# The last expert's weighting, sum and output of the last chunk in two halves, on a kernel whose order is planned

## The chip, the cores and the metric

One core of a Trainium2 chip runs the whole kernel. The time is the device time of one execution in microseconds (us). It is given as the median of several runs. A trace is one profiled execution, whose span goes from the first to the last recorded instruction.

The engines are named as the profile names them: PE is TensorE (matrix multiplies and transposes; PEld is its weight load), DVE is VectorE, ACT is ScalarE, POOL is GpSimd, and SP is SyncE, which here only issues DMAs. Each engine runs its own queue of instructions in order and waits on semaphores for the others. A "q" behind a name (SPq, ACTq) means the engine's sequencer, for instance while it issues a DMA.

## What is computed

The input is x with two batches, 1024 steps and 128 channels. Four layers follow, each behind a layer normalization and added to x:

```python
x = x + attn_a(layernorm(x))   # a linear recurrence with a decay per channel
x = x + ffn(layernorm(x))
x = x + attn_b(layernorm(x))   # 16 heads with an 8x8 state, MLPs in front and behind
x = x + ffn(layernorm(x))      # the same weights again
```

The part that the change touches is the second ffn, a dense mixture of 8 experts with 512 inner features. Every token runs through every expert:

```python
router_probs = softmax(x @ w_router)
gate_weights = softmax(x @ w_gating / 0.1)
h = silu(einsum('bsh,ehf->ebsf', x, w_gate)) * einsum('bsh,ehf->ebsf', x, w_up)
expert_out = einsum('ebsf,efh->ebsh', h, w_down)
cw = router_probs * gate_weights
cw = cw / (cw.sum(-1) + 1e-9)
out = einsum('ebsh,bse->bsh', expert_out, cw)
```

## The kernel before, in words

**Chunks and layers.** Time is cut into five chunks: four of 192 steps and a last one of 256. Both batches lie side by side, so a chunk is 384 columns wide, the last one 512. The residual x of a chunk stays in SBUF as `k.x`, with 128 tokens on the partitions and one slot of 128 channels for each block of tokens: three slots in the first four chunks, four in the last. In the last chunk two slots belong to each batch. Each chunk passes attn A, the first ffn (f), attn B and the second ffn (g). Attn B's recurrence runs step by step through its chunks on DVE, POOL and ACT, beside the experts, which keep PE busy. `ORDER` (line 84) names the sequence of experts: F0 to F4, then G0 to G4, so g4 is the last work of the kernel.

**One ffn.** `gating` (line 1096) normalizes and transposes x to channels on partitions, makes the experts' weights cw and writes them to DRAM. `experts` (line 1152) takes each expert in four slices of 128 inner features. For one slice PE makes gate and up, each with three matmuls in split precision (`mm3`, line 807), in two PSUM tiles; ACT applies Silu to the gate; DVE (for some slices POOL) multiplies it with up; and PE multiplies the result by the down weights (`down`, line 1159), three slices behind. Gate, up and the down sum share four PSUM tiles ("g", `PSG`). After an expert's fourth slice, `add(e)` (line 1170) reads the broadcast weight `cb` by DMA and multiplies the expert's result with it into a tile `de` (`ds` for expert 0). For most experts that is a copy on ACT and a product on POOL; for the last expert it is one DVE product from PSUM. The products are summed in `ds`.

**The end of g4.** `APART` (line 117) holds "g4". There the sum of experts 0 to 6 is transposed back to tokens on partitions and added to `k.x` by itself (lines 1185 to 1187), beside the last expert's matmuls. The last expert's product is then transposed in four blocks (`transposed`, line 992, line 1192) and added (line 1193). `store` (line 1593) issues one output DMA for each batch of the chunk, as `blocks` (line 765) yields them, both on SP's queue.

**Who sets the order.** No engine call in the kernel's body emits an instruction at once. `Program` (lines 369 to 677) records each call as a step with its engine, its tiles and the steps it depends on, and a list scheduler (`order`, line 486) then simulates the engines with a price list of its own (`_cost`, lines 425 to 484) and picks, for each engine, the ready step of lowest rank. All instructions are emitted from line 677, so every row of the profile carries L677, and rows are told apart by their tiles. The rank is:

```python
far[s.index] = tail(s) + max([far[o.index] for o in s.after], default=0.0)
s.rank = -far[s.index] - s.lead + spread * s.index
```

`far` is the step's longest path to the end of the program at the planner's prices. The lead is a table by part and chunk (`LEAD`, line 71), the spread 427.5 ns for each place in the recorded order. The price of a DVE product or sum of n columns is n / 0.96 + 145 ns (line 452), so 678 for 512 columns and 412 for 256; a transpose of 128 columns is 112 + 195 = 307.

**Which steps depend on which.** Two steps depend on each other where one writes what the other touches. In SBUF the planner compares the ranges within a tile. For a PSUM tile that TensorE and another engine use it takes the whole tile (lines 413 to 417):

```python
for o, ow, olo, ohi, om in tile.steps:
    if (w or ow) and o is not s:
        if psum and "T" in (o.engine, s.engine):
            s.deps.add(o)
        elif lo < ohi and olo < hi and om & m:
            s.deps.add(o)
```

The names in the profile: `g_at` is one of the four PSUM tiles of gate, up and down; `m_at` one of the two other PSUM tiles; `h_at` the Silu and the product; `de_at`, `ds_at`, `cb_at` as above; `x_at` the residual; `wgu_at`, `wd_at` experts' weights; `Zt_at`, `y_at`, `ox_at`, `ot_at`, `pm_at`, `q_at`, `bu_at`, `pz_at`, `xne_at`, `s_de_at`, `s_kr_at` belong to attn B.

Of the kernel before, what the change touches and what calls it, by code (L numbers as in the profile page):

```python
# [35 lines left out]
ALU = mybir.AluOpType  # L36
# [4 lines left out]
E, FF = 8, 512  # L41
EH = 153
ET = EH - 128
P = 128
# [72 lines left out]
APART = "g4".split()  # L117
# [563 lines left out]
def hybrid_kernel(  # L681
# [21 lines left out]
    nc = Program(tc.nc)  # L703
# [21 lines left out]
    def psum(name, w=W, ring=None):  # L725
        pool, tag = ring or ((ps_e, "e" if PSE else "m") if late[0] else (ps_m, "m"))
        return pool.tile([P, W], F32, tag=tag, name=name)[:, 0:w]
# [9 lines left out]
    def chunk(c, t0, tc):  # L737
        k = SimpleNamespace(c=c, t0=t0, tc=tc, w=B * tc, nt=B * tc // P)
        k.qt = tc // 4
        k.ns = k.qt // L  # L740
        k.nseg = 4 * k.ns
        return k

    chunks = [chunk(c, sum(CHUNKS[:c]), tc) for c, tc in enumerate(CHUNKS)]
# [11 lines left out]
    ident = cst[:, 0:P]  # L756
# [8 lines left out]
    def blocks(k, far):  # L765

        for b in range(B):
            q, end = b * k.tc, (b + 1) * k.tc
            while q < end:
                p, n = q % P, q // P  # L770
                t = k.t0 + q - b * k.tc
                m = (end - q) // P
                if p == 0 and m:
                    yield k.x[:, n : n + m, :], far[b, t : t + m * P, :].rearrange("(n p) d -> p n d", p=P)
                    q += m * P
                else:
                    r = min(P - p, end - q)
                    yield k.x[p : p + r, n, :], far[b, t : t + r, :]
                    q += r
# [27 lines left out]
    def mm3(to, w, v, start=True, stop=True):  # L807
        (wh, wl), (vh, vl) = w, v
        nc.tensor.matmul(to, wl, vh, start=start, stop=False)
        nc.tensor.matmul(to, wh, vl, start=False, stop=False)  # L810
        nc.tensor.matmul(to, wh, vh, start=False, stop=stop)
# [23 lines left out]
    def expert_stage(e):  # L835
        st = early(f"wst_{e}", [P, 2, FF])
        nc.sync.dma_start(st[:, 0], w_gate[e])
        nc.sync.dma_start(st[:, 1], w_up[e])
        return st

    def expert_weights(e, f, name, stage):

        t = w2p.tile([P, 2, 2, P], F32R, tag="wgu", name=f"wgu_{name}_{e}_{f}", bufs=NWGU)
        if (e, f) in wcut:
            nc.sync.dma_start(t.bitcast(F32), wcut[e, f])
            return t
        src = stage[:, :, f * P : (f + 1) * P]
        nc.scalar.copy(t[:, 0], src)
        nc.vector.tensor_tensor(t[:, 1], src, t[:, 0].bitcast(F32), ALU.subtract)
        wcut[e, f] = dram.tile([P, 2, 2, P], F32, name=f"wcut_{e}_{f}", bufs=1)  # L850
        nc.sync.dma_start(wcut[e, f], t.bitcast(F32))
        return t

    def down_weights(e, name):

        src = w_down[e].rearrange("p (k h) -> p k h", k=4)
        t = w2p.tile([P, 4, C], F32, tag="wd", name=f"wd_{name}_{e}")
        nc.sync.dma_start(t, src)
        return t
# [76 lines left out]
    def either(site, usual):  # L936

        return nc.vector if vector(site, usual) else nc.gpsimd

    def vector(site, usual):  # L940
        SITES[site] = usual
        return (usual == "V") != (site in ENG)
# [49 lines left out]
    def transposed(k, src, name):  # L992

        pt = psum(f"pt_{name}", k.w)
        for n in range(k.nt):
            nc.tensor.transpose(pt[:, n * P : (n + 1) * P], src[:, n, :], ident)
        return pt

    def tiles(k, ap):
        return ap.rearrange("p (n d) -> p n d", n=k.nt)  # L1000
# [151 lines left out]
    def experts(k, name, gated):  # L1152

        w = k.w
        xc, weight = gated
        queue = []
        s = SimpleNamespace(done=0, pd=None, sum=None)

        def down():
            wt, h = queue.pop(0)  # L1160
            f = s.done % 4
            if f == 0:
                s.pd = ps_d.tile([P, W], F32, tag=DT, name=f"pd_{name}_{s.done // 4}")[:, 0:w]
            nc.tensor.matmul(s.pd, wt, h, start=f == 0, stop=f == 3)
            s.done += 1
            if f == 3:
                with nc.ahead(AHEAD):
                    add(s.done // 4 - 1)

        def add(e):  # L1170

            cb = weight(e)
            d = w2p.tile(
                [P, W], F32, tag="de" if e else "ds", name=f"de_{name}_{e}", bufs=NDE if e else 1
            )[:, 0:w]
            if vector(f"dm_{name}{e}", "V" if e == E - 1 else "P"):
                nc.vector.tensor_tensor(d, s.pd, cb, ALU.mult)
            else:
                nc.scalar.copy(d, s.pd)
                nc.gpsimd.tensor_tensor(d, d, cb, ALU.mult)  # L1180
            if e == 0:
                s.sum = d
            elif e < E - 1:
                either(f"ds_{name}{e}", "P").tensor_tensor(s.sum, s.sum, d, ALU.add)
                if e == E - 2 and name in APART:
                    po = transposed(k, tiles(k, s.sum), f"d{name}s")
                    nc.vector.tensor_tensor(k.x, k.x, tiles(k, po), ALU.add)
            else:
                if name not in APART:
                    nc.vector.tensor_tensor(s.sum, s.sum, d, ALU.add)  # L1190
                    d = s.sum
                po = transposed(k, tiles(k, d), f"d{name}")
                nc.vector.tensor_tensor(k.x, k.x, tiles(k, po), ALU.add)

        for e in range(E):
            nc.part = name.upper()
            stage = None if (e, 0) in wcut else expert_stage(e)
            wd = down_weights(e, name)
            for f in range(4):
                wt = expert_weights(e, f, name, stage)  # L1200
                pg = psum(f"pg_{name}_{e}_{f}", w, (ps_g, GT))
                mm3(pg, (wt[:, 0, 0], wt[:, 1, 0]), xc)
                pu = psum(f"pu_{name}_{e}_{f}", w, (ps_g, GT))
                mm3(pu, (wt[:, 0, 1], wt[:, 1, 1]), xc)
                h = w2p.tile([P, W], F32, tag="h", name=f"h_{name}_{e}_{f}", bufs=NH)[:, 0:w]
                with nc.ahead(AHEAD):
                    nc.scalar.activation(h, pg, AF.Silu)
                    if 4 * e + f in HPOOL.get(name, ()):
                        u = w2p.tile([P, W], F32, tag="h", name=f"u_{name}_{e}_{f}", bufs=NH)[:, 0:w]
                        nc.scalar.copy(u, pu)  # L1210
                        nc.gpsimd.tensor_tensor(h, h, u, ALU.mult)
                    else:
                        nc.vector.tensor_tensor(h, h, pu, ALU.mult)
                    queue.append((wd[:, f, :], h))
                if len(queue) > BEHIND:
                    down()
            if e == E - 1:
                while queue:
                    down()
            nc.part = ""  # L1220
            yield
# [369 lines left out]


    def store(k):
        for tiled, steps in blocks(k, out):
            nc.sync.dma_start(steps, tiled)

    gated, rec, res = {}, {}, {}
    made = {("X", 0): 1}
# [93 lines left out]
    for name in ORDER:  # L1692
        layer, k = name[0].lower(), chunks[int(name[1])]
        ensure(layer, k.c)
        for _ in experts(k, f"{layer}{k.c}", gated[layer, k.c]):
            now += 1
            give()
        made[layer.upper(), k.c] = 1
        give()
        if layer == "g":  # L1700
            store(k)
# [68 lines left out]
```

## Time and profile before

| what | value |
|---|---|
| median of 3 runs | 769.29 us (767.77 to 771.74) |
| the profiled execution's own time | 767.02 us |
| its span, first to last instruction | 765.2 us |
| mean granted TensorE clock | 0.984 |
| PE busy | 718.2 us, 94% of the span |
| DVE busy | 605.8 us, 79% |
| ACT busy | 457.8 us, 60% |
| POOL busy | 430.7 us, 56% |
| DMA | 152.11 MB, mean 199 GB/s |
| activation table loads on ACT | 64, 1283 ns each |

How to read it. A busy share is a mean over stages with different limits, so the page also cuts the span into 40 equal slices and gives each engine's share of a slice in tenths. The chain that ended last is followed back from the last instruction; its shares say which engine's work, not which engine's waiting, leads to the end. In rows of the timeline an idle time ahead of an instruction stands in brackets, with what ended it. Two short views complete the table. The largest waits of PE (what was waited for, us in total, times, longest):

```profile
engine line waited for: us in total, times, longest us
PE g_at L677 <- ACT h_at L677: 9.5, 9, 5.4
PE m_at L677 <- DVE xn_at L677: 8.9, 2, 8.0
PE g_at L677 <- DVE h_at L677: 8.2, 11, 2.3
PE m_at L677 <- DVE bias_at L677: 3.0, 1, 3.0
PE g_at L677 <- POOL h_at L677: 2.3, 1, 2.3
```

And the two stretches in which the granted clock fell in the middle of the kernel (window, length, busy us and count of PE, PEld, DVE, ACT, POOL, granted clock, DMA share, GB/s):

```profile
405.60:409.00 3.40, 0.73 (x6) 0.41 (x4) 3.40 (x4) 3.00 (x8) 2.00 (x2) 1.00 0.71 196
409.00:412.40 3.40, 0.62 (x2) 0.62 (x3) 3.37 (x9) 3.08 (x10) 3.32 (x6) 0.50 0.44 108
412.40:415.80 3.40, 3.40 (x13) 2.68 (x12) 3.40 (x9) 0.98 (x2) 0.23 (x1) 0.50 0.16 34
467.00:470.40 3.40, 1.58 (x6) 0.94 (x6) 3.37 (x13) 3.37 (x6) 3.24 (x7) 1.00 0.41 103
470.40:473.90 3.50, 2.48 (x4) 1.40 (x5) 3.50 (x8) 3.48 (x6) 3.50 (x5) 0.51 0.31 109
473.90:477.30 3.40, 3.39 (x9) 1.90 (x7) 3.04 (x7) 3.13 (x6) 3.40 (x4) 0.50 0.00 0
477.30:480.70 3.40, 3.35 (x22) 3.23 (x23) 3.35 (x9) 2.19 (x4) 3.09 (x5) 1.00 0.38 83
```

### The profile page before, as it was taken

What the parts mean: (1) busy time and instruction counts of PE and PEld (TensorE: products, weight loads), DVE (VectorE), ACT (ScalarE), POOL (GpSimd) and SP (SyncE); (2) the same over time, 40 slices, a digit from 0 to 9 for tenths busy, and PEclk for the clock granted to TensorE, in tenths of its full rate; (3) what the DMA queues carried; (4) which work ended last, traced back from release to release, by engine and by line L of the source; (5) the groups of instructions that cost most, each with busy time, mean ns of one, the idle gap of its engine ahead of it and who ended that gap; (6) DMA issues with size and microseconds to landing.
All of it is one profiled execution on the core that took longest, in us unless ns stands there. A gap on an engine that the chain in (4) does not pass through costs nothing.

```text
span 765.2 us, 11738 instructions
## 1 busy us (share of the span) xinstructions
PE 718.2 (94%) x3231; PEld 553.7 (72%) x3231; DVE 605.8 (79%) x1387; ACT 457.8 (60%) x913; POOL 430.7 (56%) x490
## 2 busy tenths in 40 slices
PE   4799999899999999999997988999999999999997
PEld 3788887778777878656655755778777777776664
DVE  6675744699999999899999999999999778344332
ACT  3665577648774775643877969655654553554332
POOL 2232332886545497655975589975976247520222
PEclk9799999999999999999998998999999999999999
DMA  7487568676976589855395693686658857746551
GB/s 230 154 286 257 160 182 213 211 207 192 221 216 198 175 218 284 225 169 172 120 235 154 180 311 108 189 257 211 199 179 249 258 163 221 238 134 192 177 166 42
DMA packets 131559, 152.11 MB, mean 199 GB/s; under 512 B 52950, under 2 KB 74518, under 8 KB 131494
## 3 DMA queue, kind: packets, MB, share of 16 engines
q1 hardware_dynamic: 130918, 150.98, 66.8%
q8 instruction: 26, 0.43, 0.2%
q10 hardware_dynamic: 576, 0.38, 0.2%
q14 instruction: 39, 0.32, 0.1%
HBM read 131.79 MB, written 19.53 MB: 198 GB/s over the span
## 4 chain that ended last, share of the span: by engine, by line
PE 46%; DVE 24%; DMA 7%; POOL 7%; issue 6%; ACT 6%; SPq 2%; DVEq 0%; ACTq 0%; POOLq 0%
PE g_at L677 40%; PE m_at L677 7%; DVE h_at L677 5%; DVE bu_at L677 2%; POOL ox_at L677 2%; ACT L677 2%; DVE Z_at L677 2%; DVE pz_at L677 2%; DVE q_at L677 2%; SPq L677 2%; DMA wgu_at<-wcut 2%; ACT h_at L677 1%; DMA d_v<-b_at 1%; DVE ot_at L677 1%; POOL pm_at L677 1%
## 5 line engine op out<-in xcount | busy, mean ns | idle before, releaser
L677 PE MATMUL g_at<-xT_hi_at,wgu_at 128*128 128x384 f32 (+1 forms) x1280 | 483.9, 417 | 16.4 <-ACT h_at L677 9.0
L677 PEld LDWEIGHTS g_at<-xT_hi_at,wgu_at 128*128 128x128 f32 x1280 | 240.1, 190 | 84.1 <-ACT h_at L677 17.5
L677 PE MATMUL g_at<-h_at,wd_at 128*128 128x384 f32 (+1 forms) x640 | 269.1, 512 | 5.5 <-DVE h_at L677 2.7
L677 ACT ACTIVATE h_at<-g_at 128x384 f32<-128x384 f32 (+1 forms) x320 | 162.7, 512 | 185.5 <-PE g_at L677 171.4
L677 DVE TENSOR_TENSOR h_at<-h_at,g_at 128x384 f32<-128x384 f32 (+1 forms) x302 | 172.4, 574 | 98.9 <-PE g_at L677 55.3
L677 PE MATMUL g_at<-xT_lo_at,wgu_at 128*128 128x384 f32 (+1 forms) x640 | 226.6, 354 | 0.0
L677 PEld LDWEIGHTS g_at<-xT_lo_at,wgu_at 128*128 128x128 f32 x640 | 122.3, 191 | 38.9 <-issue 12.5
L677 PEld LDWEIGHTS g_at<-h_at,wd_at 128*128 128x128 f32 x640 | 116.6, 190 | 27.2 <-DVE h_at L677 5.0
L677 POOL TENSOR_TENSOR de_at<-de_at,cb_at 128x384 f32<-128x384 f32 (+1 forms) x50 | 54.8, 1096 | 90.3 <-ACT de_at L677 90.3
L677 ACT ACT_TABLE_LOAD x64 | 82.1, 1283 | 3.7 <-issue 2.6
L677 POOL TENSOR_TENSOR ds_at<-ds_at,de_at 128x384 f32<-128x384 f32 (+1 forms) x58 | 66.3, 1143 | 24.6 <-DVE de_at L677 22.7
L677 POOL TENSOR_TENSOR Z_at<-Z_at,vr_at 128x192 f32<-128x192 f32 (+1 forms) x75 | 49.5, 660 | 34.8 <-DVE Z_at L677 31.7
L677 ACT COPY Zt_at<-Z_at 128x384 f32<-128x384 f32 (+1 forms) x40 | 39.1, 981 | 9.7 <-DVE Z_at L677 7.7
L677 DVE TENSOR_TENSOR q_at<-bu_at,kt_at 128x384 f32<-128x384 f32 (+1 forms) x75 | 43.7, 583 | 0.7
L677 DVE TENSOR_REDUCE bu_at<-pz_at 128x48 f32<-128x384 f32 (+1 forms) x75 | 43.3, 577 | 0.6
L677 POOL TENSOR_TENSOR ox_at<-Zt_at,y_at 128x384 f32<-128x384 f32 (+1 forms) x36 | 40.9, 1152 | 4.8 <-DVE y_at L677 4.6
L677 DVE TENSOR_TENSOR Z_at<-Z_at,q_at 128x384 f32<-128x384 f32 (+1 forms) x75 | 42.8, 571 | 0.8
L677 DVE TENSOR_TENSOR pz_at<-Z_at,bu_at 128x384 f32<-128x384 f32 (+1 forms) x75 | 42.8, 570 | 0.4
L677 ACT COPY de_at<-g_at 128x384 f32<-128x384 f32 (+1 forms) x50 | 24.9, 499 | 27.7 <-PE g_at L677 26.1
L677 POOL TENSOR_TENSOR vr_at<-vt_at,rks_at 128x384 f32<-128x384 f32 (+3 forms) x40 | 35.3, 886 | 1.1
L677 POOL TENSOR_TENSOR om_at<-Z_at,rst_at 128x384 f32<-128x384 f32 (+1 forms) x25 | 32.2, 1286 | 3.6 <-DVE Z_at L677 3.6
L677 POOL TENSOR_TENSOR h_at<-h_at,h_at 128x384 f32<-128x384 f32 x18 | 18.3, 1016 | 17.2 <-ACT h_at L677 17.2
(223 smaller groups left out, 973.0 us busy)
## 6 DMA issues: line engine op xcount, KB each, us to landing
wgu_at<-wcut SPq DMA_DIRECT2D x288, 256.0 KB, 3.1
wd_at<-in_w_down SPq DMA_DIRECT2D x80, 256.0 KB, 2.9
wcut<-wgu_at SPq DMA_DIRECT2D x32, 256.0 KB, 3.8
cb_at<-cd_f SPq DMA_DIRECT2D x32, 192.0 KB, 4.2
cb_at<-cd_g SPq DMA_DIRECT2D x32, 192.0 KB, 3.4
Z_at<-in_w_gate SPq DMA_DIRECT2D x8, 256.0 KB, 2.8
Z_at<-in_w_up SPq DMA_DIRECT2D x8, 256.0 KB
cb_at<-cd_f SPq DMA_DIRECT2D x8, 256.0 KB
```

Source lines behind the costliest of these rows:

```text
L677: getattr(engine, s.call)(*[placed(v) for v in s.args], **{n: placed(v) for n, v in s.kw.items()})
```

## The change

For the last expert of the last chunk of g, `add` no longer multiplies the whole 128x512 result, transposes its four blocks and adds them. It takes one PSUM tile for the transposes and goes through the two batches: for each it multiplies a half (128x256) on DVE, transposes its two blocks and adds the half to `k.x`. `store` sends the second output DMA of the last chunk from ACT's queue instead of SP's. Nothing else in the text of the kernel changes; the order of all steps is planned anew from the recorded ones.

```diff
@@ -1173,6 +1173,16 @@
             d = w2p.tile(
                 [P, W], F32, tag="de" if e else "ds", name=f"de_{name}_{e}", bufs=NDE if e else 1
             )[:, 0:w]
+            if e == E - 1 and k is chunks[-1] and name in APART:
+
+                po = psum(f"pt_d{name}", w)
+                for i in range(2):
+                    ts = slice(i * k.nt // 2, (i + 1) * k.nt // 2)
+                    nc.vector.tensor_tensor(tiles(k, d)[:, ts], tiles(k, s.pd)[:, ts], tiles(k, cb)[:, ts], ALU.mult)
+                    for n in range(ts.start, ts.stop):
+                        nc.tensor.transpose(po[:, n * P : (n + 1) * P], d[:, n * P : (n + 1) * P], ident)
+                    nc.vector.tensor_tensor(k.x[:, ts], k.x[:, ts], tiles(k, po)[:, ts], ALU.add)
+                return
             if vector(f"dm_{name}{e}", "V" if e == E - 1 else "P"):
                 nc.vector.tensor_tensor(d, s.pd, cb, ALU.mult)
             else:
@@ -1591,8 +1601,8 @@
 
 
     def store(k):
-        for tiled, steps in blocks(k, out):
-            nc.sync.dma_start(steps, tiled)
+        for i, (tiled, steps) in enumerate(blocks(k, out)):
+            (nc.scalar if k is chunks[-1] and i % 2 else nc.sync).dma_start(steps, tiled)
```

## The prediction

> **What bounds the kernel now.** I read the page's slices first, to see which engine fills which stage, then the chain that ended last, then windows of 40 us. The slices (each digit tenths of 19.1 us):
>
> ```profile
> PE   4799999899999999999997988999999999999997
> ...
> DVE  6675744699999999899999999999999778344332
> ...
> PEclk9799999999999999999998998999999999999999
> ...
> PE 46%; DVE 24%; DMA 7%; POOL 7%; issue 6%; ACT 6%; SPq 2%; DVEq 0%; ACTq 0%; POOLq 0%
> ```
>
> PE is full nearly throughout; DVE is full from 160 to 560 us; only two dips of PE and of its clock stand in the middle. The windows that decide below (columns: window, its length, busy us and count of PE, PEld, DVE, ACT, POOL, granted clock, DMA share, GB/s):
>
> ```profile
> 400.00:440.00 40.00, 34.32 (x152) 26.36 (x151) 39.28 (x93) 33.60 (x66) 21.22 (x28) 0.91 0.60 175
> 440.00:480.00 40.00, 34.42 (x144) 24.33 (x142) 39.14 (x82) 32.77 (x54) 37.56 (x42) 0.91 0.69 205
> 480.00:520.00 40.00, 38.80 (x181) 30.38 (x182) 39.29 (x87) 23.42 (x52) 33.79 (x33) 1.00 0.78 229
> 520.00:560.00 40.00, 39.10 (x189) 30.81 (x187) 39.70 (x80) 24.77 (x46) 30.85 (x30) 1.00 0.62 193
> 640.00:680.00 40.00, 37.95 (x186) 30.86 (x185) 19.76 (x42) 19.58 (x38) 24.28 (x28) 1.00 0.70 211
> ```
>
> From 440 to 560 us DVE idles 0.86 + 0.71 + 0.30 = 1.87 us in all, so a DVE delay there is not won back. After 640 DVE has 20 of 40 us free, PE 2.05. What the diff names is the end alone (start, us, engine, tile, count, idle before and its releaser):
>
> ```profile
> 759.70 0.69 DVE L677 TENSOR_TENSOR de_at<-g_at,cb_at 128x512 f32<-128x512 f32 x1 [2.73 <-PE g_at L677]
> 760.31 0.68 DVE L677 TENSOR_TENSOR x_at<-x_at,m_at 128x512 f32<-128x512 f32 x1
> ...
> 760.45 0.66 PE L677 MATMUL m_at<-cst_at,de_at 128*128 128x128 f32 x4 [0.40 <-DVE de_at L677]
> 761.14 0.69 DVE L677 TENSOR_TENSOR x_at<-x_at,m_at 128x512 f32<-128x512 f32 x1 [0.15 <-PE m_at L677]
> 761.86 0.90 SPq L677 DMA_DIRECT2D out_x<-x_at  x2
> ```
>
> Weighting, four transposes, sum, two stores in single file; the second store starts 0.44 us after the first (762.30), and the span ends at 765.2, 2.9 us after that. The whole tail the diff can shorten is 765.2 - 759.7 = 5.5 us, 0.7% of the span.
>
> **Part 1: the tail itself.** A DVE row of 128x384 takes 0.55 us and of 128x512 0.69, a slope of 0.14 for 128 elements, so 128x256 is about 0.41. Independent rows overlap by 0.08 (759.70 + 0.69 against 760.31), so two halves start 0.33 apart. The chain after: first mult 759.70 to 760.11, second 760.03 to 760.44; the other experts' sum into x stands behind both on DVE, 760.36 to 761.04; two transposes (0.4 of the 0.66) 760.17 to 760.57; the first half's sum 761.05 to 761.46; its store on SP at 761.49, 0.37 earlier than now. The second half's transposes: the planner counts a PSUM tile as one whole when TensorE and another engine use it (lines 413 to 417), so they wait not only for the second mult but for DVE's first sum; in the built program their wait is on that sum. They run 761.52 to 761.92, the second sum 761.95 to 762.36, the second store on ScalarE's queue at 762.39, where ScalarE has nothing left (its issues at the kernel's start took 0.41 to 0.45, SP's two here 0.39 and 0.46). That is 762.39 against 762.30: **+0.1 us**. Without that wait the two sums would follow each other and the second store go at about 761.85: **-0.45**. With an ACT issue and a wait hop each 0.25 longer: +0.6. I take +0.1: the halves run one after the other, and what the parallel issue saves (0.44) the serial second half gives back. Nothing is queued behind the waiting transposes or the second store.
>
> In the row at 760.31 DVE reads one PSUM tile while PE writes another. No row shows both at once in one tile. The Trainium skill ("PSUM — Partial Sum Buffer", section "PSUM bank collisions raise a hardware error") says that two engines in one bank at once fail rather than queue, which speaks for the wait and against halves in one tile; by it the -0.45 is not to be had without a second tile.
>
> **Part 2: what the tail does to the rest.** The order of all instructions is planned by the kernel: a step's rank (line 503) is minus its longest path to the end, by its own price list (lines 425 to 484). By that list the path from the sum of the other experts to the end was 678 + 678 ns and is now 678 + 412 + 307 + 412, so 453 ns longer. Everything whose longest path runs into the last chunk (its attention, hence all chunks' recurrences) gains 453 ns of urgency against the experts of g0 to g3. In the two built programs PE, DVE, ACT, POOL and SP are identical up to about 414 us of the trace; from there hundreds of places differ on each; they meet again from 561 to 600, and from 692 to the tail. The work is the same but for two DVE halves (+0.3 us in all) and one activation table load (x64 at 1283 ns becomes x65).
>
> To price the new order I gave each instruction the mean duration of its kind in the trace and compared how much work stands ahead of the same instruction in both. That leaves out waits, so it bounds a delay rather than giving it. Two stretches stand out.
>
> *450 to 485 us.* ACT now:
>
> ```profile
> 449.69 0.48 ACT L677 ACTIVATE h_at<-g_at 128x384 f32<-128x384 f32 x1
> 450.37 0.48 ACT L677 COPY h_at<-g_at 128x384 f32<-128x384 f32 x1 [0.19 <-PE g_at L677]
> 451.48 0.49 ACT L677 ACTIVATE h_at<-g_at 128x384 f32<-128x384 f32 x1 [0.63 <-PE g_at L677]
> ```
>
> After the Silu of 449.69 the new order puts a table load (1.28), an Exp of the decay (0.5), two Zt copies (1.87), two PSUM copies (0.96), a third Zt copy (0.92), three xne (1.15), a Square (0.5) and the table load back (1.28): 8.5 us, so the Silu of 451.48 cannot start before 458.6. PE covers some of it with attention matmuls and the four PSUM tiles that gates and ups share, then stands. It stands already now, with waits of
>
> ```profile
> 457.93 0.91 PE L677 MATMUL g_at<-h_at,wd_at 128*128 128x384 f32 x2 [2.28 <-POOL h_at L677]
> 467.43 0.44 PE L677 MATMUL g_at<-xT_hi_at,wgu_at 128*128 128x384 f32 x1 [0.52 <-ACT h_at L677]
> 471.42 2.29 PE L677 MATMUL g_at<-h_at,wd_at 128*128 128x384 f32 x3 [2.29 <-DVE h_at L677]
> ```
>
> so the question is the net. On PE both orders meet at the matmul of 471.42: the same work ahead of it. Its delay is the stretch's delay. Its product, at 463.4 on DVE now, has 8.6 us more DVE work ahead (472.0 + 0.57 = 472.6), its Silu, at 460.60 on ACT, 9.2 us more: at 469.8 if ACT never waits. ACT idles 7.2 and DVE 0.9 of these 40 us, and if ACT waits 2 us in that stretch the matmul starts at 474.6. So +1.2 to +3.2; after it DVE, full until 560, keeps the loss. I take **+2.5**, above the middle because the sum of works leaves waits out; for the range 0 (the Silus after it catch up) to +5 (the decay's data, whose load is issued at 442.20, lands late and holds DVE too).
>
> In the rows PE fell to clock 0.50 from 409.0 to 415.8 and from 470.4 to 477.3, after windows with PE busy 0.73 and 1.58 of 3.4 us, and not after 648.0 to 651.4 with 1.71. Half clock for 6.9 us costs about 3.4. The Trainium skill ("TensorE: Matmul & The Clock Gate", section "Part 1: The HAM clock gate") puts the gate on a free-running window of about 3.4 us, idle or busy; by it the stall that moves here can meet one window more or fewer, 3.4 us either way. My sum keeps one such stretch, as now.
>
> *620 to 652 us.* DVE now runs two products at 624.1 and 624.7; the new order puts 3.5 to 4.9 us of attention work (two 1.2 us rows and the router's small ones) ahead of each, 1.1 by 633.4. PE's cover is what the four shared tiles let it run ahead, one to two slices of an expert; a slice takes 1.74 us (23 records of the down matmul from 500 to 520 us, two to a matmul, as 640 records for 320 slices show). The middle, 4.2 - 2.6, leaves 1.6. At 647.57 a DVE row of 3.67 and one of 0.68 now stand before a product that they followed, so PE's 2.05 wait ending at 651.76 grows by about a slice, 1.7. The two are not added: that row hangs on POOL and DVE, not on the experts, so a PE that is 1.6 late waits 1.6 less for it. **+1.6**; bounds 0 (all covered) and +4 (added, and 0.7 for waits).
>
> *The rest.* 500 to 556 us: products have up to 2.0 us less ahead, but DVE is full and its total is the same: 0. 414 to 450: up to 4.4 more ahead, 0 again by 481: within the first stretch's bounds. The added table load is among the 8.5. SP's issues move with the rest (0.3 to 0.6 each); I price that at 0, since no wait of PE over 0.2 us in the list of waits names a DMA, and DMA is busy 0.69 there; if a load came late it would be in the +5.
>
> **Sum.** +2.5 +1.6 +0.1 = +4.2 us. On the profiled execution's 767.02 that is 771.2; that execution is 2.27 below the median of the runs, 769.29, and on the median it is **773.5 us**, +0.55%.
>
> **Rivals.**
> - *The tail works and the rest is hidden.* Both stretches at 0, the tail between -0.45 and +0.6: 768.8 to 769.9. For it: PE's count of work is the same and both orders meet twice. Against: 8 us on ACT where PE already waits.
> - *The new order takes the stall away* (the other side: faster). If the attention work done early on ACT and DVE at 450 to 461 lets PE pass 467 to 471 without the waits of 0.52 and 2.29, no window falls idle and the half clock of 470.4 to 477.3 goes: -2.8 - 3.4 + 0.1 = -6.1, 763.2. It decides as soon as that product is ready by 469.1, 2.3 us before it is needed now. Against: it has 8.6 us more DVE work ahead, not less.
> - *One half-clock stretch more* on top of my sum: +3.4, 776.9; with all upper bounds (+5, +4, +0.6) 778.9.
> - *The change doesn't do what it says*: the halves do not overlap and the second queue saves nothing. That is already my tail.
>
> **How the numbers follow.** Forecast (delays stand, +0.6 to +7) 0.55; hidden 0.22; stall gone 0.13; more half clock 0.10. A measurement of this kernel tells about 0.5%, 3.85 us. Of the forecast's 0.55 I put 0.40 above that bound. Slower 0.40 + 0.10 = 0.50; same 0.15 + 0.22 = 0.37; faster 0.13. The range goes from 765.0 (both stretches at 0, one half-clock stretch lost, the tail at -0.45: 765.4, rounded down) to 780.0 (the upper bounds and 1 us of the runs' own spread); it leaves out the stall-gone case and half of the last, 0.18.
>
> **What would show it.** Tail: the second half's transposes wait on DVE's x, the second store starts on ACT 2.7 us after the first mult starts (2.6 now). Stretch 1: no Silu between 450.2 and 458.6, a PE wait on ACT of over 2 us there, the 471.42 matmul at 472.6 to 474.6. Stretch 2: a new PE wait on DVE's products near 626 of 1 to 2 us. I am wrong if the 561 us rows come at their old times, or if PE's clock stays 1.00 through 470 to 478.

## The result and the profile after

The changed kernel took 772.92 us (median of 12 runs, 768.68 to 775.17) against 769.89 for the kernel before in the same comparison (12 runs, 766.03 to 772.43): ratio 1.004, 95% interval 1.0021 to 1.0059. It is about 3 us slower. Its profiled execution is its fastest run (768.68, span 766.9), so that page shows less of a loss than the median.

The windows of 40 us that answer to those of before (window, length, busy us and count of PE, PEld, DVE, ACT, POOL, granted clock, DMA share, GB/s); the last line is the kernel before in the window that matters most:

```profile
440.00:480.00 40.00, 34.97 (x152) 25.67 (x151) 39.42 (x87) 33.21 (x53) 37.00 (x42) 0.91 0.68 206
...
600.00:640.00 40.00, 35.02 (x161) 26.34 (x160) 33.72 (x80) 20.35 (x39) 12.13 (x14) 0.96 0.59 178
640.00:680.00 40.00, 39.95 (x196) 32.52 (x195) 20.79 (x45) 20.05 (x39) 27.52 (x28) 1.00 0.70 223
...
600.00:640.00 40.00, 38.52 (x190) 30.59 (x189) 33.50 (x84) 22.47 (x43) 15.15 (x16) 1.00 0.69 209
```

From 440 to 480 us PE's busy time shows no loss: it is even 0.55 us higher. The hole is at 600 to 640 us, where PE falls from 38.52 busy us to 35.02 and its clock to 0.96. Part of it comes back at once: PE is full from 640 to 680, where before it waited 2.05 us.

The clock of 0.96 is one stretch at half clock that before has not. It follows a window in which PE was busy 1.59 of 3.4 us:

```profile
623.70:627.10 3.40, 1.59 (x6) 0.95 (x6) 3.40 (x6) 3.34 (x6) 0.64 (x1) 1.00 0.61 182
627.10:630.50 3.40, 3.20 (x9) 2.62 (x9) 3.40 (x5) 1.02 (x3) 1.72 (x1) 0.50 0.24 74
```

Half clock for 3.4 us is, as an estimate, 1.7 us of PE's work.

To follow the delay along the kernel I took the start of each down matmul in both traces and subtracted; the difference is called the lag below. At 385 us of before, ahead of the first difference, the changed kernel stands at -0.96 us: the two executions differ by chance by that much over identical orders. From there it goes to +8.14 at 461, back to -0.91 at 591, up to +7.01 at 628, and to +1.46 from 694 on. So the first stretch leaves 0.05 us behind, the second 2.37.

The tail, changed kernel (start us, us, engine, tiles, count, idle before and its releaser):

```profile
761.16 0.76 DVE L677 TENSOR_TENSOR de_at<-g_at,cb_at 128x256 f32<-128x256 f32 x2 [2.74 <-PE g_at L677]
...
761.84 1.20 DVE L677 TENSOR_TENSOR x_at<-x_at,m_at 128x512 f32<-128x512 f32 x2
...
763.09 0.44 PE L677 MATMUL m_at<-cst_at,de_at 128*128 128x128 f32 x2 [1.01 <-DVE x_at L677]
763.57 0.42 DVE L677 TENSOR_TENSOR x_at<-x_at,m_at 128x256 f32<-128x256 f32 x1 [0.53 <-PE m_at L677]
764.02 0.41 ACTq L677 DMA_DIRECT2D out_x<-x_at  x1
```

The second half's transposes wait 1.01 us on DVE's sum into x: the halves run one after the other. From the first weighting to the issue of the second output it takes 764.02 - 761.16 = 2.86 us, against 2.60 before: +0.26. From the first weighting to the end of the span it is 5.7 us (766.9 - 761.16) against 5.5 (765.2 - 759.70): +0.2.

### The profile page after: what moved, and what is told of

The parts are those of the page before. It is cut to its first block, busy times and chain, and to the rows that moved or that the text cites. A ratio compares the mean times of both kernels' runs of the same rounds, so it can differ in the third digit from the quotient of the medians.

```text
span 766.9 us, 11750 instructions
## 1 busy us (share of the span) xinstructions
PE 719.5 (94%) x3231; PEld 555.8 (72%) x3231; DVE 606.1 (79%) x1389; ACT 457.9 (60%) x914; POOL 433.8 (57%) x490
## 4 chain that ended last, share of the span: by engine, by line
PE 52%; DVE 25%; ACT 8%; DMA 7%; issue 5%; SPq 1%; POOL 1%; DVEq 0%; ACTq 0%
PE g_at L677 44%; PE m_at L677 7%; DVE h_at L677 5%; DVE bu_at L677 3%; ACT L677 3%; DVE q_at L677 2%; DVE Z_at L677 2%; DVE pz_at L677 2%; DMA wgu_at<-wcut 1%; ACT h_at L677 1%; DMA d_v<-b_at 1%; SPq L677 1%; DMA pm_at<-zd 1%; DVE ot_at L677 1%; DVE cm_at L677 1%
## 5 line engine op out<-in xcount | busy, mean ns | idle before, releaser
L677 POOL TENSOR_TENSOR Z_at<-Z_at,vr_at 128x192 f32<-128x192 f32 (+1 forms) x75 | 51.5, 687 | 32.8 <-DVE Z_at L677 32.4
L677 POOL TENSOR_TENSOR ox_at<-Zt_at,y_at 128x384 f32<-128x384 f32 (+1 forms) x36 | 39.2, 1102 | 4.2 <-DVE y_at L677 3.1
L677 POOL TENSOR_TENSOR h_at<-h_at,h_at 128x384 f32<-128x384 f32 x18 | 19.9, 1103 | 17.9 <-ACT h_at L677 17.8
```

The source lines that it names most:

```text
L677: getattr(engine, s.call)(*[placed(v) for v in s.args], **{n: placed(v) for n, v in s.kw.items()})
```

## The experiments

All ratios are to the kernel before, measured beside it; brackets hold 95% intervals. A ratio is taken over all runs of both kernels and is not the quotient of the two medians. To separate the tail from the order, three lines let a step's share of the planner's longest path be set by hand:

```diff
+        s.path = None
-            far[s.index] = tail(s) + max(...)
+            far[s.index] = (tail(s) if s.path is None else s.path) + max(...)
```

**The tail alone.** The changed text, with the paths of its steps set so that they add up to the old ones. The order is then that of before on PE and POOL throughout, and on the other engines up to the tail.

> The changed tail with the order of before everywhere else (the planner is given the old path lengths for the tail's steps). Theory R, the new order makes the time: ratio 1.000 (within 0.15%), and in the trace only the tail is longer, first weighting to second output 2.8 to 2.9 us against 2.60. Rival T, the halves and the second queue make it: ratio 1.004, the 3 us stand in the tail. Rival N, clock and chance: anything between, with nothing in the tail.

Measured: 0.9999 (0.9976 to 1.0022), and the tail is 2.86 us here too (761.81 to 764.67). The halves and the second queue cost 0.26 us up to the second output and nothing that a ratio can show. Rival T falls.

**The order alone.** The old text, with the last sum's path set to 1438 ns and the last weighting's to -202.

> The old tail with the order of the changed kernel up to it (only the urgency is changed: 760 ns added to the last sum's path, the last weighting's path corrected). Theory R: 1.003 to 1.004 (2.5 to 3 us), and the stretch 620 to 652 us shows the same new waits as in the changed kernel. Rival T: 1.000. Rival N: interval takes in both.

Measured: 1.0059 (1.0038 to 1.0079), medians 773.55 (six runs) against 768.22, and PE waits 0.62, 1.26 and 0.58 us from 628 to 634, as in the changed kernel. The new order alone makes a loss as large as the whole change's, as far as the intervals tell. Rival N falls too: the interval keeps clear of 1. Setting the paths also showed an error of mine. With the 453 ns of my prediction the planner gives another order; with +760 for the last sum and -120 for the last weighting it gives the changed kernel's on every engine up to the tail. All transposes into one PSUM tile depend on each other, so each of them is in the longest path: 678 + 678 became 678 + 412 + 2 x 307 + 412.

**One stretch at a time.** Two kernels are joined from both plans near 585 us, where each engine has emitted the same instructions in both.

```diff
+        a, b = self.planned(True), self.planned(False)
+        done = {s for s in b[0] if b[1][s] < cut}
+        one, two = (a, b) if early else (b, a)
+        out = [s for s in one[0] if s in done] + [s for s in two[0] if s not in done]
```

> Old tail; the changed kernel's order up to the place near 585 us where both orders meet, the order of before behind it. My prediction's first term: +2.5 us, ratio 1.003. What the trace of the changed kernel shows instead (6 us late at 458 to 470, made up by 485, level at 585): 1.000, within 0.8 us.

> Old tail; the order of before up to the place near 585 us, the changed kernel's order behind it. My prediction's second term: +1.6 us, ratio 1.002. What the trace of the changed kernel shows: 6.3 us late at 642, 4 of them made up by 692, +2.4 us left: 1.003. If the two stretches only cost together, both this and the first one are at 1.000 to 1.001.

Measured: the first stretch 1.0016 (0.9992 to 1.0040), 1.2 us, which doesn't exclude 0 nor +2.5; the second 1.0039 (1.0011 to 1.0066), 3.0 us. Over all traces the first stretch (lag at 591 minus lag at 385) leaves 0.05, 1.37, -0.05, 1.75, 0.16, 1.51, 2.24 and 0.68 us in eight kernels that have the new order there, mean 1.0; and 1.49, 0.13, 1.19, -0.41 and -1.55 in five that have the old one, mean 0.2. The second costs, and PE's busy time from 600 to 640 us shows it: 38.5, 37.2, 38.5, 38.3 and 37.6 us in the five traces with the old order there, 35.0, 34.7 and 34.1 in the three with the new one and nothing else moved. The lag alone would not show it in one pair of traces: from 591 to 694 us it grows by 1.87, 1.85, 0.30 and 2.93 us even in the four other traces with the old order there, by 2.37 to 6.73 in the five with the new one and the loads (below) not put back.

The half clock is part of this cost. From 600 to 640 us the mean clock is 1.00 in four of the five traces with the old order and 0.96 in the fifth. It is 0.96 or 0.91 in all eight with the new one, also in those whose loads or Silus are put back below. Over 40 us that is 1.6 or 3.6 us of PE's work (an estimate from the clock alone). No run parts it from the waits that stand ahead of it.

**Two Silus ahead.** In the changed kernel ACT reads so at the start of g3:

```profile
622.79 0.69 ACT L677 COPY si_at<-lm_at 128x128 f32<-128x128 f32 x2 [2.95 <-DMA lm_at<-sd]
623.26 0.54 ACT L677 ACTIVATE h_at<-g_at 128x384 f32<-128x384 f32 x1
623.82 1.28 ACT L677 ACT_TABLE_LOAD   x1
...
626.76 0.87 ACT L677 ACTIVATE h_at<-g_at 128x384 f32<-128x384 f32 x2
```

One Silu goes ahead of the router's table loads, where before three did. I took that order for the cause first.

```diff
+        for n in ("h_g3_0_1", "h_g3_0_2"):
+            move("S", find("S", "activation", n), seq["S"].index(find("S", "activation", "ex_g3")))
+        for n, o in (("h_g3_0_1", "h_g3_0_0"), ("h_g3_0_2", "h_g3_0_1")):
+            move("V", find("V", "tensor_tensor", n), seq["V"].index(find("V", "tensor_tensor", o)) + 1)
```

> The order-only kernel with one edit near 624 us: two Silus of g3's first expert go ahead of the router's Exps and their table load on ACT, and their two products follow the first one on DVE, as in the order of before; nothing else moves. If the second stretch's loss comes from these Silus behind the table loads (theory R in its narrow form): 1.0059 falls to about 1.003, and PE's waits of 0.6, 1.26 and 0.58 us near 628 to 634 shrink to under 1 us in all. Rival, the attention's late data hold ACT and DVE there whatever stands behind: 1.005 to 1.006, and PE waits as long at another row.

Measured: 1.0049 (1.0024 to 1.0073), and PE's waits there are 2.06, 0.58 and 1.63 us: not shorter, only at other rows. The narrow form falls by the waits; the ratio cannot tell it from 1.003. What stands first is the 2.95 us for which ACT waits on a DMA (3.67 in this kernel, 0.69 before), with the Silus behind it.

**A product of the attention on DVE.** In the changed kernel a router row of 3 columns takes as long as a POOL product beside it:

```profile
626.48 2.36 DVE L677 TENSOR_TENSOR dn_at<-su_at 128x3 f32<-128x3 f32 x1
```

```diff
+        s = find("P", "tensor_tensor", "ym_4_1")
+        seq["P"].remove(s)
+        s.engine = "V"
+        seq["V"].insert(seq["V"].index(next(o for o in seq["V"] if o.call == "tensor_reduce" and s in o.deps)), s)
```

> The order-only kernel with one product of the attention (128x1024, 2.4 us on POOL) done on DVE instead, at its place ahead of its reduction. If the router's 3-column row took 2.36 us on DVE because POOL ran that product beside it: the row takes under 0.3 us, the stretch gets 1 us shorter (2.36 - 0.17 - 1.2), ratio 1.004 to 1.005. Rival, the row waits for something else: it stays at 2.4 and the time is 1.007.

Measured: the row takes 0.16 us instead of 2.36, so the cause of its length is shown. The ratio, 1.0035 (1.0006 to 1.0065), overlaps with 1.0059; the gain of 1 us isn't told from 0.

**Two PSUM tiles for the halves, and the second queue alone** (one run, for its trace), both on the order of before.

```diff
                 for i in range(2):
+                    po = psum(f"pt_d{name}_{i}", w, (ps_g, GT) if i else None)
```

> The order of before, the tail in halves with a PSUM tile of its own for each half, so that the second half's transposes need not wait for the first sum. My working of the tail: first weighting to second output about 2.15 us, 0.45 less than before's 2.60 and 0.7 less than the changed kernel's 2.86; ratio 0.9995, not to be told from 1. Rival, DVE's queue is what serialises the halves and the wait was only its shadow: 2.6 us or more.

> Before with the second output alone moved to ScalarE's queue. My working: the two issues start together instead of 0.44 us apart, first weighting to last issue 2.16 to 2.2 us against 2.60, and the span ends about 0.4 us sooner after it. Rival, the issue is not what the end waits for (the writes of both outputs share the same DMA engines): the issue moves but the span ends as long after the last sum as before, 3.4 us.

Measured: with two tiles 2.24 us from first weighting to second output, the transposes of the second half starting 0.42 us after those of the first, without a wait on DVE; ratio 1.0011 (0.9985 to 1.0038), not told from 1. With the second queue alone both issues start at 763.65, 2.16 us after the weighting, but the span ends 3.2 us later instead of 2.9: from the weighting to the end 5.4 us against 5.5 before, about 0.1 gained of 0.44. Here the rival was right for most of it: what follows the issue, not the issue, sets the end. The Trainium skill ("DMA: Bandwidth & Descriptors", section "Issuing engines are not separate DMA queues") says that DMAs from several engines run on the same 16 DMA engines and that only issue time is saved; the 0.1 us agrees, and even that time was saved only in part.

**Two weight loads on SP's queue.** What feeds ACT's 2.95 us wait stands on SP, changed kernel:

```profile
614.77 0.33 SPq L677 DMA_DIRECT2D wd_at<-in_w_down  x1
615.79 0.32 SPq L677 DMA_DIRECT2D sd<-S_at  x1
...
618.48 0.33 SPq L677 DMA_DIRECT2D wd_at<-in_w_down  x1
619.56 1.74 SPq L677 DMA_DIRECT2D lm_at<-sd  x4
```

The same store and loads in the kernel before, and ACT's row behind them:

```profile
614.99 0.32 SPq L677 DMA_DIRECT2D sd<-S_at  x1
...
617.11 1.74 SPq L677 DMA_DIRECT2D lm_at<-sd  x4
...
620.41 0.67 ACT L677 COPY si_at<-lm_at 128x128 f32<-128x128 f32 x2 [0.69 <-DMA lm_at<-sd]
```

The attention's state is stored (sd) and loaded again (lm). In the order of before each of the two `wd_at` rows follows the state's row beside it, and the loads go 2.12 us after the store (614.99 to 617.11). Now the second `wd_at`, which must wait for its buffer, stands ahead of the loads, and they go 3.77 us after it. In this one trace the weight load holds them until 618.81; the last 0.75 us is a wait for the store itself to land (SP's waits name sd). In the other four traces with this order, apart from the swap below, they follow the weight load at once, 3.12 or 3.13 us after the store. Three kernels move these two issues, the third with the two Silus as well:

```diff
+        move("D", wd[1], load[-1])
+        move("D", wd[0], save)
```

> The order-only kernel with two DMA issues put back on SP's queue: the two loads of down weights, which the new order put ahead of the store of the attention's state and ahead of its four loads, go behind them as in the order of before. Nothing else moves. New theory: the second of these weight loads waits for its buffer and holds the state's loads behind it on SP, 3.1 us from store to load against 1.8 to 2.1 in the order of before. If so, that distance returns to about 2, ACT's wait for the loaded state falls by 1 to 2 us, and the ratio falls from 1.0059 to about 1.004. Rival, the chain that makes the state is itself late and the loads only follow: the distance returns, the time does not.

> Before, with only these two DMA issues swapped as in the new order. If the swap alone is enough: store to load grows from 2 to 3 us or more, ACT's Silus behind the state's copies start 1 to 2 us later, and the ratio is 1.001 to 1.002. Rival, the slack of PE there hides it: 1.000, with the distance grown all the same.

> Both mends together: the loads back on SP's queue, and the two Silus and products ahead of the router's Exps. If the second stretch's loss is the sum of these two orders (queue of SP, queue of ACT): 1.002 to 1.003, and PE's lag at 690 us over that at 590 falls from 3.3 us to 1 or less. Rival, what is left in DVE's order (the attention's rows ahead of later products) makes it: 1.005.

Measured: with the loads back the distance returns to 1.76 us and the ratio is 1.0024 (0.9999 to 1.0049). With the swap put into the kernel before, the distance grows to 3.80 us, ACT waits 3.45:

```profile
622.43 0.66 ACT L731 COPY si_at<-lm_at 128x128 f32<-128x128 f32 x2 [3.45 <-DMA lm_at<-sd]
```

and the ratio is 1.0030 (1.0001 to 1.0058): two places exchanged on a queue that only issues DMAs cost 2.3 us by themselves (0.1 to 4.5). That interval only just clears 1, and it is one of a dozen here; in its profiled execution the lag grew by 2.84 us from 591 to 694, against 2.93 in the trace in which only the second output's queue was changed. The two directions agree (0.3% to 0.35%), but the interval of the kernel with the loads back overlaps with 1.0059, and in its profiled execution the second stretch still left 3.26 us, with half clock from 630 to 635. Both mends together gave 1.0021 (0.9997 to 1.0045), no more than the loads alone; in that profiled execution the lag still grew by 4.9 us, where 1 was expected.

What the swap does to the queues is shown: in all traces the loads go 3.12 to 3.80 us after the store with it (six traces) and 1.76 to 2.12 without (eight), and ACT waits 2.3 to 3.7 us for them with it and at most 0.9 without. That it costs time is likely, not certain. That it is all of the second stretch is refuted by PE: with the loads back, here and in the mended kernel below, ACT's wait is gone, yet PE is busy only 35.3, 34.2 and 35.3 us from 600 to 640 and the half clock is still there (0.91, 0.91 and 0.96). With the swap alone it is 36.4 us at a clock of 1.00. What else in the new order holds PE stays open. A candidate that no run tests is the attention's rows on DVE: with both mends DVE runs no expert's product between 630.1 and 639.1 us, where PE waits on ACT and DVE.

**The changed kernel mended** by two tiles and by the loads put back.

> The changed kernel with two mends: a PSUM tile of its own for each half of the tail (paths kept, so the order elsewhere stays the new one), and the two weight loads back behind the state's store and loads on SP's queue. If these two are what the change costs: the tail 2.24 us as with two tiles (against 2.86), and the ratio 1.004 falls to 1.000 to 1.002. Rival, the rest of the new order (ACT and DVE near 624 us) keeps the cost: 1.003 to 1.005.

Measured: 1.0025 (1.0003 to 1.0046), between the two expectations; the tail took 2.24 us. It overlaps with 1.004, so a gain is not shown, and no version here beats the kernel before. Taken together, the three kernels with the loads back stand at 1.0021 to 1.0025 and the five with the new second stretch and the loads not back at 1.0035 to 1.0059. So the loads are probably worth something, and what is left with them back is about as large.

## Why the prediction was right in sum and wrong in parts

- **The direction and the size.** Forecast +4.2, measured +3.0 (1.6 to 4.5). The mechanism that I put first, a new order made by the planner and not the tail, is shown by the first two experiments. That the sum is near is partly luck: the first term was 1.3 to 1.5 us too large and the second, by its middle value, 1.4 too small.
- **The signs of being wrong.** Both that I had named came in the changed kernel's trace. The rows near 561 us come at nearly their old times (lag -0.85 us there, -0.96 at 385; over the eight traces with the new order they are 0.0 to 2.3 us late). The clock stays 1.00 from 470 to 478, in all eight. So the first stretch did not do what I forecast, though the sum did.
- **The tail.** Forecast +0.1, measured +0.26. The serial halves were right. Mis-sized was mostly the way to the second transposes: 1.93 us from the first weighting (761.16 to 763.09), where I had 1.82. My -0.45 without the wait was 0.36 with two tiles (2.24 against 2.60).
- **453 ns.** Wrong: it is +760 for the last sum and -120 for the last weighting, as told above. The places where the orders differ were read from the programs, so the sum did not hang on it.
- **450 to 485 us.** Here the step that failed is "after it DVE, full until 560, keeps the loss". The step ahead of it held: no Silu between 450.2 and 458.73 (forecast 458.6), PE waits of 2.28 and 1.85 us, and the matmul of 471.42 comes 2.3 to 4.2 us late in the eight traces with the new order, against the lag at 385 us (forecast 1.2 to 3.2). But two thirds of it are gone by 591. DVE did not idle through PE's stall (39.42 of 40 us busy against 39.14): the new order had given it attention work to do meanwhile. So I now count DVE's idle time, not a late product, as the loss where DVE is the bound; no run tests that reading by itself. The term is 1.0 from the traces and 1.2 from the ratio, not 2.5. The half clock moved but did not go: 6.8 us up to 463.2 (clock 0.86, 0.50 and 0.64 in the three windows of 3.4 us from 454.0) instead of 470.4 to 477.3.
- **The matmul of 471.42.** What releases it was misread. The product that this matmul reads was done at 463.92 in the trace before, 7.5 us ahead of it; what ended PE's 2.29 us wait was the next product on DVE, 470.81 to 471.36. In the changed kernel the matmul's own product is done at 470.17 (found by the order of the program) and the matmul starts at 472.84, behind a Silu on ACT. So my 472.6, built on its own product, came near for another reason. My upper end of 474.6 doesn't follow from its own numbers either: a Silu at 469.8 + 2 ends at about 472.3 and a product behind it at 472.9.
- **620 to 652 us.** Forecast +1.6, measured 3.0 (0.9 to 5.1), so the size is not shown to be wrong. PE's new waits of 0.60, 1.26 and 0.58 us stand near 625, 627 and 631. The forecast had one of 1 to 2 us on DVE's products; only the 0.60 is on DVE, the others are on ACT. Two prices are missing. One is "SP's issues move with the rest (0.3 to 0.6 each); I price that at 0, since no wait of PE over 0.2 us in the list of waits names a DMA": the DMA that came late feeds ACT, and PE's list cannot name it. The swap alone made ACT wait 3.45 us instead of 0.69 and measured 2.3 us (0.1 to 4.5). The other is "My sum keeps one such stretch, as now": the changed kernel's trace has one half-clock stretch more, 3.4 us from 627.1. And the forecast that PE's 2.05 us wait near 652 grows was wrong: it is gone. With it go 1.8 of the 6.1 us by which PE is late at 642 (counted from 591), and another 2.3 come back between 681 and 694.
- **The rivals.** "The rest is hidden" is excluded by the order alone. "The new order takes the stall away": the one of 470 us went, but one as long came at 456, and no time was won. "One half-clock stretch more" came in half the size that I gave it, 3.4 us or about 1.7 of PE's work instead of 3.4.

## What to carry to other kernels

Where a scheduler orders the whole program, a change to its last few instructions is a change to all that leads there: keep the old order by force and time the edit and the order apart. Compare the queue that only issues DMAs as closely as the engines: here one issue that waited for its buffer held the issues behind it (3.12 to 3.80 us from store to loads instead of 1.76 to 2.12), and the price showed as a wait of the engine that the later DMA feeds. Count a stall on the engine that bounds the stretch, and add the half clock that may follow it. A wait that disappears is not yet time won: ACT's did, and PE's hole stayed.

## What the runs showed of the hardware

A DVE row of three columns took 2.36 us while POOL multiplied two SBUF tiles, and 0.16 without. The Trainium skill ("SBUF — State Buffer", section "SBUF: two separate sides") says that DVE with two SBUF inputs and POOL share one pair of ports by an exclusive lock held for the whole instruction; both rows agree (POOL's took 2.36 us as well, from 626.46).

The clock answers unevenly to the same wait. Before's wait of 2.05 us near 650 left it at 1.00 (first line). In the kernel with the first stretch alone the same wait, in a window with less of PE's work in it, was followed by half clock (the other two):

```profile
648.00:651.40 3.40, 1.71 (x9) 1.13 (x7) 3.40 (x2) 0.98 (x2) 2.41 (x3) 1.00 0.94 254
...
647.40:650.80 3.40, 1.35 (x6) 1.12 (x5) 3.30 (x4) 0.49 (x1) 0.94 (x1) 0.87 0.67 249
650.80:654.20 3.40, 3.40 (x12) 2.58 (x10) 0.00 (x0) 1.30 (x3) 1.97 (x2) 0.63 0.60 212
```

The lag in that trace grew by 1.6 us there. Two executions of one order can thus differ by as much as the effect under study, and a single profile shows where time goes but not how much.
